# Second bias of the experts gathered into the output rows by an indirect DMA, in place of a matmul

## The chip, the cores and the metric

The kernel runs on one core of one Trainium2 chip. The metric is the device time of one execution in microseconds (us). Engines are named as in the profile: PE is TensorE's matmuls and PEld its weight loads, DVE is VectorE, ACT is ScalarE, POOL is GpSimd, SP is SyncE; a "q" behind a name (POOLq) is the engine's own queue of waits, register and DMA-issuing instructions.

## The reference, cut to what matters

1250 tokens of 1024 features go through a two-layer graph network (two SAGE layers over 40000 edges) and then through a feed-forward part with eight experts, of which each token takes the best two. The change lies in the last part:

```python
logits = jax.nn.silu(t @ rw1 + rb1) @ rw2 + rb2
vals, idx = jax.lax.top_k(logits, K)                       # K = 2 of E = 8 experts
w = jax.nn.softmax(masked, axis=1)                         # zero but for the two
eh = jax.nn.silu(jnp.einsum('td,edh->teh', t, ew1) + eb1[None])
eo = jnp.einsum('teh,ehd->ted', eh, ew2) + eb2[None]       # eb2: 8 x 1024, the second bias
y = t + jnp.einsum('te,ted->td', w, eo)
```

`x + y` is returned. So a token's row receives, for each of its two experts, w * (silu(t @ ew1 + eb1) @ ew2 + eb2). All is float32.

## The kernel before

**The first 925 us** are the graph network and the router: nearly all of it is matmuls, written with their own orders and buffers. The change touches it only where the second bias is prepared. In `routing_constants` (L266) eb2 is loaded as 64 x 128 values and split into three bfloat16 parts that add up to the float32 value (L297 and L299, three copies and two subtractions on DVE); each part is stored to a scratch tensor `eb2_d` in DRAM (L300). A constant `ones_b` of 3 x 128 ones is set (L302). Just before the experts start, the three parts are loaded into three partitions, `eb2_r` (L1599, on ACT's queue).

**The experts.** The 2 x 1250 (token, expert) pairs are sorted by expert into tiles of 128 slots, every tile of one expert; with this input there are 23 tiles. For each tile i there are two integer lists, `ids` (which token row each slot reads) and `to` (which output row it adds to), an expert number in `eid[:, i]`, the same in all partitions, and a weight per slot, `w_slot`. One tile goes through these steps:

- `gather(i)` (L1470): an indirect DMA from POOL reads the 128 token rows of 4 KB from `t_d` in DRAM into one of three buffers `xgs`.
- `fetch(i)` (L1481, L1482): PE turns the eight 128 x 128 blocks, ACT copies them from PSUM in two halves of 128 x 512.
- `first_layer(i)` (L1486 to L1498): PE and ACT load the expert number into a register (L1486), PE multiplies by ew1 (L1493), DVE copies the result (L1498).
- `second_layer(i)` (L1505 to L1529): PE turns the two halves of that result (L1505), ACT applies Silu with the first bias (L1507), and then for each half of the 1024 columns PE adds the bias by a matmul of `ones_b` with the three parts (L1514) and two products with ew2 (L1518) in one PSUM tile. The first half is weighted and copied out by ACT (L1524), the second by DVE (L1526), into one of two buffers `yos[i % 2]`. An indirect DMA from POOL adds the 128 rows to their rows of `out` in DRAM (L1529); below this is called the scatter of tile i.

The buffers `xgs`, `yos` and the turned tokens lie in columns of one large SBUF tensor L that the router has finished with. All indirect DMAs are issued by POOL in its own queue, one after the other. A scatter waits until the scatter before it has landed, since both add to `out`; and a tile's output buffer is written again two tiles later, when its scatter has landed.

**Order of the work.** `section` (L1543) writes, for each i, gather(i + 3), fetch(i + 1), first_layer(i), second_layer(i - 1). A scheduler may move instructions within each engine, and does: in the built kernel, in the regular stretch, PE goes first layer, the two turns of the tile before (L1505), its two bias matmuls (L1514), one turn of a token block, its second layer (L1518), the other seven turns. Each engine executes its own list in order. Tiles 0 to 19 are always there; tiles from 20 on lie in nested branches (`sections`).

The rest of the routing (`plan_rest`, L1419) is computed by DVE while tiles 0 to 2 run.

Of the kernel before, what the change touches and what calls it, by code (L numbers as in the profile page):

```python
# [13 lines left out]
BF = mybir.dt.bfloat16  # L14
I32 = mybir.dt.int32
AF = mybir.ActivationFunctionType
ALU = mybir.AluOpType
# [4 lines left out]
P = 128  # L22
# [6 lines left out]
def kernel(  # L29
# [21 lines left out]
    nc = tc.nc  # L51
    N, D = x.shape
    NE = src.shape[0]
    E, _, H = ew1.shape
    KD = D // P
    KH = H // P
# [22 lines left out]
    const = ctx.enter_context(tc.tile_pool(name="const", bufs=1))  # L79
    small = ctx.enter_context(tc.tile_pool(name="small", bufs=3))  # L80
    land = ctx.enter_context(tc.tile_pool(name="land", bufs=1))
    dram = ctx.enter_context(tc.tile_pool(name="dram", bufs=1, space=bass.MemoryType.DRAM))
    tpp = ctx.enter_context(tc.tile_pool(name="tpp", bufs=2, space=PSUM))
    t_d = dram.tile([NP, D], F32, name="t_d")
    v_d = dram.tile([NP, D], F32, name="v_d")
    eb2_d = dram.tile([3, E * D], BF, name="eb2_d")


    NT = KD * N
    WQ = KD * QW  # L90
    L = land.tile([P, NT + 4 * D + 2 * WQ], F32, name="L")
    hT1 = L[:, :NT].rearrange("p (k n) -> p k n", k=KD)
    SC = L[:, NT : NT + 4 * D]
    WW = L[:, NT + 4 * D :]
# [47 lines left out]
    stt = nc.vector.scalar_tensor_tensor  # L142
# [26 lines left out]
    at_iota = [9440]  # L169

    def iota(shape, pattern, mult=0):

        n = 1
        for d in shape[1:]:
            n *= d
        ti = L[: shape[0], at_iota[0] : at_iota[0] + n].bitcast(I32)
        at_iota[0] += n
        assert at_iota[0] <= NT - 320
        if len(shape) == 3:
            ti = ti.rearrange("p (a b) -> p a b", b=shape[2])  # L180
        nc.gpsimd.iota(ti, pattern=pattern, base=0, channel_multiplier=mult)
        return ti

    def counted(ti, name, dtype=F32):
        tf = const.tile(list(ti.shape), dtype, name=name)
        tc.keep_in_program_order(nc.vector.tensor_copy(tf, ti))
        return tf
# [76 lines left out]
    need = {}  # L264

    def routing_constants():  # L266
        late = tc.keep_in_program_order
        tiles = counted(tiles_i, "tiles")
        token = counted(token_i, "token")
        own_row = counted(own_row_i, "own_row")  # L270
        first = counted(first_i, "first")
        late(nc.vector.tensor_scalar(first, first, 0.0, None, op0=ALU.is_gt))

        lower = const.tile([P, P], F16, name="lower")
        late(nc.vector.tensor_scalar(lower, lane, own_row, None, op0=ALU.is_gt))
        ones = const.tile([P, P], F16, name="ones")
        late(nc.vector.memset(ones, 1.0))
        valid = const.tile([P, NB], F32, name="valid")
        late(nc.vector.tensor_scalar(valid, token, float(N), None, op0=ALU.is_lt))

        late(nc.vector.tensor_scalar(token, token, 1.0, None, op0=ALU.add))
        late(nc.vector.tensor_mul(token, token, valid))
        rb1_p = const.tile([P, KD], F32, name="rb1_p")
        late(nc.sync.dma_start(out=rb1_p, in_=rb1.rearrange("(k p) -> p k", p=P)))
        rb2_p = const.tile([E, 1], F32, name="rb2_p")
        late(nc.sync.dma_start(out=rb2_p, in_=rb2.rearrange("(e o) -> e o", o=1)))
        eb1_p = const.tile([P, E, KH], F32, name="eb1_p")
        late(nc.sync.dma_start(out=eb1_p, in_=eb1.rearrange("e (k p) -> p e k", p=P)))
        rw2_sb = const.tile([P, KD, E], F32, name="rw2_sb")
        late(nc.sync.dma_start(out=rw2_sb, in_=rw2.rearrange("(k p) e -> p k e", p=P)))  # L290

        ev = L[: E * D // P, NT - 320 : NT]
        eb2_f = ev[:, :P]
        late(nc.sync.dma_start(out=eb2_f, in_=eb2.rearrange("e (a n) -> (e a) n", n=P)))
        for i in range(3):
            part = ev[:, P + i * (P // 2) : P + (i + 1) * (P // 2)].bitcast(BF)
            late(nc.vector.tensor_copy(part, eb2_f))  # L297
            if i < 2:
                late(nc.vector.tensor_tensor(eb2_f, eb2_f, part, ALU.subtract))  # L299
            late(nc.sync.dma_start(out=eb2_d[i].rearrange("(a n) -> a n", n=P), in_=part))  # L300
        ones_b = const.tile([3, P], BF, name="ones_b")
        late(nc.vector.memset(ones_b, 1.0))  # L302
        lg = const.tile([P, NB, E], F32, name="lg")
        late(nc.vector.memset(lg, 0.0))
        need.update(
            tiles=tiles, token=token, first=first, lower=lower, ones=ones, valid=valid,
            rb1_p=rb1_p, rb2_p=rb2_p, eb1_p=eb1_p, rw2_sb=rw2_sb, ones_b=ones_b, lg=lg,
        )


# [696 lines left out]
    def moe():  # L1007
# [1 line left out]
        tiles, token, first, lower, ones, valid = (  # L1009
            need[k] for k in ("tiles", "token", "first", "lower", "ones", "valid")  # L1010
        )
        rb1_p, rb2_p, eb1_p, rw2_sb, ones_b, lg = (
            need[k] for k in ("rb1_p", "rb2_p", "eb1_p", "rw2_sb", "ones_b", "lg")
        )
        xwp = st.enter_context(tc.tile_pool(name="xwp", bufs=1, side="right"))
        xw = xwp.tile([P, E * WEXP], F32, name="xw")
# [42 lines left out]
        late = carver(SC[:, 512:1792])  # L1059
# [8 lines left out]
        def column(k):  # L1068
            return hT1[:, k, :TA]
# [3 lines left out]
        yos = [column(4 + i) for i in range(2)]  # L1073
# [12 lines left out]
        ids, to, eid = (keep([P, NTILE], I32) for _ in range(3))  # L1086
        w_slot = keep([P, NTILE])
# [375 lines left out]

        w1_all = xw.rearrange("p (e w) -> p e w", e=E)[:, :, : KD * H]
        w2_all = xw.rearrange("p (e w) -> p e w", e=E)[:, :, KD * H :]
        eb2_r = WW.bitcast(BF)[:3, : E * D]
        eb2_e = eb2_r.rearrange("i (e d) -> i e d", e=E)

        def gather(i):
            nc.gpsimd.indirect_dma_start(  # L1470
                out=xgs[i % 3], out_offset=None, in_=t_d[:N, :],
                in_offset=bass.IndirectOffsetOnAxis(ap=ids[:, i : i + 1], axis=0),
            )

        def fetch(i):
# [9 lines left out]
        def first_layer(i, xT):  # L1485
            e = nc.values_load(  # L1486
                eid[0:1, i : i + 1], engines=(ENG.PE, ENG.Activation),
                min_val=0, max_val=E - 1,
                skip_runtime_bounds_check_because="eid is a count of experts, cut at E - 1",
            )  # L1490
            ps = mm.tile([P, 512], F32, name="ps")
            for k in range(KD):
                nc.tensor.matmul(  # L1493
                    ps[:, :H], xT[:, k, :], w1_all[:, ds(e, 1), k * H : (k + 1) * H],
                    start=(k == 0), stop=(k == KD - 1),
                )
            hx = hxs[i % 2]
            nc.vector.tensor_copy(hx, ps[:, :H])  # L1498
            return e, hx

        def second_layer(i, e, hx):
            pt = tpp.tile([P, 4, P], F32, name="tp")
            hT = hTs[i % 2]
            for q in range(KH):
                nc.tensor.transpose(pt[:, q, :], hx[:, q * P : (q + 1) * P], ident)  # L1505
            for q in range(KH):
                nc.scalar.activation(  # L1507
                    hT[:, q, :], pt[:, q, :], AF.Silu, bias=eb1_p[:, ds(e, 1), q : q + 1]
                )
            yo = yos[i % 2]  # L1510
            for h in range(2):
                dc = slice(h * HALF, (h + 1) * HALF)
                ps = mm2.tile([P, 512], F32, name="ps2")
                nc.tensor.matmul(  # L1514
                    ps, ones_b, eb2_e[:, ds(e, 1), dc], start=True, stop=False
                )
                for q in range(KH):
                    nc.tensor.matmul(  # L1518
                        ps, hT[:, q, :],
                        w2_all[:, ds(e, 1), q * D + h * HALF : q * D + (h + 1) * HALF],  # L1520
                        start=False, stop=(q == KH - 1),
                    )
                if h == 0:
                    nc.scalar.activation(yo[:, dc], ps, AF.Copy, scale=w_slot[:, i : i + 1])  # L1524
                else:
                    nc.vector.tensor_scalar(  # L1526
                        yo[:, dc], ps, w_slot[:, i : i + 1], None, op0=ALU.mult
                    )
            nc.gpsimd.indirect_dma_start(  # L1529
                out=out[:, :],  # L1530
                out_offset=bass.IndirectOffsetOnAxis(ap=to[:, i : i + 1], axis=0),
                in_=yo, in_offset=None, bounds_check=N - 1, oob_is_err=False,
                compute_op=ALU.add,
            )
# [48 lines left out]
        for c in range(LAST):  # L1583
            logits(c)
        at_a, take_a = plan_first()
        gather(0)
        gather(1)
        gather(2)
        route(w2, 2, LAST)
# [6 lines left out]
        logits(LAST)  # L1596
        lgp.close()
        mm2 = st.enter_context(tc.tile_pool(name="mmy", bufs=3, space=PSUM))
        nc.scalar.dma_start(out=eb2_r, in_=eb2_d[:, :])  # L1599
        xTs[0] = fetch(0)  # L1600
        xTs[1] = fetch(1)
        held[0] = first_layer(0, xTs.pop(0))
        gather(3)
        section(1, 2, until=always)
# [52 lines left out]
```

## Time and profile before

| | |
|---|---|
| median of 3 runs | 1163.0 us (1160.78 to 1163.17) |
| the profiled execution | 1160.5 us |
| its span, first to last instruction | 1158.6 us |
| mean granted TensorE clock | 0.993 |
| PE busy | 1122.4 us, 97% of the span |
| POOL busy | 331.3 us, 29% |
| ACT busy | 181.5 us, 16% |
| first token gather issued | 924.97 us |
| last scatter issued | 1146.44 us |

Times in the profile count from the first instruction. A row of a group gives line, engine, operation, output<-inputs, shapes and the number of instructions, then busy us and mean ns of one, then the idle time of the engine just before them and what ended it. For a DMA on POOL the busy time is only that of POOL's own work of issuing it; the data moves later, and "to landing" is the time from the start of the issue until the transfer is complete. Matmuls overlap in the pipeline, so the mean duration of one is longer than the distance from one to the next. The line numbers are those of the kernel before.

### The profile page before, as it was taken

How to read it: one execution, taken by the hardware profiler on the slowest of the kernel's cores; microseconds unless marked ns; L12 is line 12 of the kernel's file. 1: busy time of each engine (PE TensorE's matmuls, PEld its weight loads, DVE VectorE, ACT ScalarE, POOL GpSimd, SP SyncE). 2: the span in 40 equal slices, each digit the busy share in tenths (PEclk: the TensorE clock that was granted, in tenths of full speed). 3: DMA queues.
4: the chain of work that ended last, by engine and by line, in shares of the span. 5: the costliest groups of instructions: out<-in, count | busy, mean ns of one | idle time of the engine just before them, and what ended most of it. 6: DMA issues, size and time to landing. Idle time of an engine off the chain costs nothing.

```text
span 1158.6 us, 13209 instructions
## 1 busy us (share of the span) xinstructions
PE 1122.4 (97%) x4775; PEld 789.3 (68%) x4775; DVE 452.2 (39%) x1127; ACT 181.5 (16%) x420; POOL 331.3 (29%) x438
## 2 busy tenths in 40 slices
PE   6999999999999999999999999999999989999994
PEld 4556556888888886887788688865333666666662
DVE  8767778751212164241234142555221532111110
ACT  5301000001111111100110000122111223222220
POOL 1899999700000000031004011540000013323221
PEclk9999999999999999999999999999999999999997
DMA  7011011010100021042014432347801435554542
GB/s 230 32 40 39 1 37 37 1 37 1 37 1 1 1 73 37 10 170 72 1 34 164 167 118 73 145 164 257 279 19 36 146 89 132 107 121 101 126 116 45
DMA packets 59330, 95.40 MB, mean 82 GB/s; under 512 B 8797, under 2 KB 35645, under 8 KB 59251
## 3 DMA queue, kind: packets, MB, share of 16 engines
q1 hardware_dynamic: 48400, 67.72, 17.0%
q0 software_dynamic: 7056, 23.88, 9.1%
q10 hardware_dynamic: 3798, 2.84, 0.8%
q8 instruction: 42, 0.69, 0.2%
q14 instruction: 34, 0.28, 0.1%
HBM read 68.76 MB, written 27.47 MB: 83 GB/s over the span
## 4 chain that ended last, share of the span: by engine, by line
PE 94%; DVE 2%; ACT 1%; DMA 1%; POOL 1%; issue 0%; ACTq 0%; DVEq 0%; POOLq 0%
PE ps L524 12%; PE ps L458 11%; PE psb L638 9%; PE ps L708 8%; PE ps L560 8%; PE ps L638 7%; PE ps L1493 7%; PE ps L1518 7%; PE ps L1173 5%; PE ps L625 5%; PE ps L1186 4%; PE cnt L419 3%; PE ps L1128 2%; PE tp L1481 2%; PE lg L1105 2%; PE ps L1514 1%
## 5 line engine op out<-in xcount | busy, mean ns | idle before, releaser
L409 POOL TENSOR_SCALAR ol<-lane,keys 125x128 f16<-125x128 f16 x320 | 192.1, 619 | 27.7 <-DVE oh L416 27.7
L458 PE MATMUL ps<-h0T,L 128*128 128x498 f32 (+2 forms) x384 | 147.6, 517 | 0.3 <-ACT h0T L321 0.2
L524 PE MATMUL ps<-L,h0T 128*128 128x256 f32 (+1 forms) x640 | 142.2, 379 | 0.0
L704 POOL TENSOR_TENSOR L<-L 128x512 f32<-128x512 f32 (+1 forms) x20 | 32.0, 1608 | 375.6 <-DVE L L617 217.6
L524 PEld LDWEIGHTS ps<-L,h0T 128*128 128x128 f32 (+1 forms) x640 | 118.3, 187 | 18.0 <-issue 0.6
L416 DVE TENSOR_SCALAR oh<-win,keys 125x240 f16<-125x240 f16 x320 | 85.7, 322 | 30.9 <-PE cnt L419 29.1
L458 PEld LDWEIGHTS ps<-h0T,L 128*128 128x128 f32 x384 | 67.5, 192 | 39.0 <-issue 33.9
L1493 PE MATMUL ps<-xw,L 128*128 x368 | 84.7, 383 | 0.3 <-issue 0.3
L1518 PE MATMUL ps<-xw,L 128*128 x184 | 83.5, 596 | 0.1
L560 PE MATMUL ps<-C,yh 128*128 128x256 f32 (+2 forms) x240 | 81.8, 356 | 0.0
L560 PE MATMUL ps<-C,yl 128*128 128x256 f32 (+2 forms) x240 | 81.5, 353 | 0.0
L708 PE MATMUL ps<-zh,C 128*128 128x512 f32 (+1 forms) x200 | 79.5, 398 | 0.0
L708 PE MATMUL ps<-zl,C 128*128 128x512 f32 (+1 forms) x200 | 78.6, 393 | 0.0
L1493 PEld LDWEIGHTS ps<-xw,L 128*128 128x128 f32 x368 | 69.0, 192 | 10.1 <-issue 1.4
L1529 POOL DMA_INDIRECT out_dram<-L x23 | 36.3, 1579 | 133.4 <-ACT L L1482 87.9
L1470 POOL DMA_INDIRECT L<-t_d,L x26 | 26.0, 1000 | 162.2 <-DVE L L140 142.2
L438 DVE TENSOR_TENSOR C<-C,cnt 128x240 f32 x160 | 64.4, 402 | 13.4 <-DVE oh L416 2.1
L1518 PEld LDWEIGHTS ps<-xw,L 128*128 128x128 f32 x184 | 33.2, 190 | 35.3 <-issue 33.0
L140 DVE TENSOR_TENSOR L<-L,ps 128x512 f32<-128x512 f32 (+1 forms) x28 | 17.1, 611 | 99.7 <-PE ps L1173 47.2
L419 PEld LDWEIGHTS <-ol 125*128 125x128 f16 x320 | 31.0, 97 | 36.6 <-POOL ol L409 21.7
L419 PE MATMUL cnt<-oh,ol 125*128 125x240 f16 x320 | 50.8, 265 | 2.5 <-POOL ol L409 2.1
L1526 DVE TENSOR_SCALAR L<-ps,L 128x512 f32<-128x512 f32 x23 | 17.3, 751 | 91.7 <-PE ps L1518 91.7
(224 smaller groups left out, 1516.6 us busy)
## 6 DMA issues: line engine op xcount, KB each, us to landing
xw<-in_L_ffn_ew_dram SPq DMA_DIRECT2D x16, 1024.0 KB, 7.6
L<-in_x_dram SPq DMA_DIRECT2D x20, 256.0 KB, 2.9
v_d<-L SPq DMA_DIRECT2D x18, 256.0 KB, 2.0
xa<-v_d SPq DMA_DIRECT2D x18, 256.0 KB, 5.9
t_d<-L SPq DMA_DIRECT2D x9, 512.0 KB, 4.4
out_dram<-xa SPq DMA_DIRECT2D x9, 512.0 KB, 4.0
L<-in_L_gnn_W_self_dram SPq DMA_DIRECT2D x4, 1024.0 KB, 5.7
L<-in_L_gnn_W_neigh_dram SPq DMA_DIRECT2D x4, 1024.0 KB
```

The source lines that it names most:

```text
L409: nc.gpsimd.tensor_scalar(ol[:, c, :], lane[:GP], keys[:, 1, c, r : r + 1], None, op0=ALU.is_equal)
L416: nc.vector.tensor_scalar(oh, win[:GP], keys[:, 0, i * GC + c, r : r + 1], None, op0=ALU.is_equal)
L419: nc.tensor.matmul(ps[:, i, :GW], ol[:, i * GC + c, :], oh, start=(c == 0), stop=(c == GC - 1),)
L438: nc.vector.tensor_tensor(to, to.bitcast(F32), ps[:, i, :GW].rearrange("p (k w) -> p k w", k=NB), ALU.add,)
L458: nc.tensor.matmul(ps[:, :n], w[:, k, (d % 2) * P : (d % 2 + 1) * P], h0T[:, k, c0 : c0 + n], start=(k == 0), stop=(k == KD - 1),)
L524: nc.tensor.matmul(ps[:m, :QW], hT[:, k, blk(b)], w[:, k, :], start=(k == 0), stop=(k == KD - 1))
L560: nc.tensor.matmul(ps[:, :n], part[: rows[k], k, (d % 2) * P : (d % 2 + 1) * P], C[: rows[k], k, c0 : c0 + n], start=(k == 0 and part is y ...
L625: nc.tensor.matmul(ps[:m], hT1[:, k, blk(b)], w[:, k, :], start=(k == 0), stop=(k == KD - 1))
L638: nc.tensor.matmul(ps, rows_of(k), w[:, k, :], start=(first and k == 0), stop=(k == KB - 1), skip_group_check=not first,)
L708: nc.tensor.matmul(ps[:m], C[: rows[k], k, blk(b)], part[: rows[k], k, :], start=(k == 0 and part is yh), stop=(k == NB - 1 and part is yl),)
L1493: nc.tensor.matmul(ps[:, :H], xT[:, k, :], w1_all[:, ds(e, 1), k * H : (k + 1) * H], start=(k == 0), stop=(k == KD - 1),)
L1518: nc.tensor.matmul(ps, hT[:, q, :], w2_all[:, ds(e, 1), q * D + h * HALF : q * D + (h + 1) * HALF], start=False, stop=(q == KH - 1),)
```

## The change

The second bias is no longer part of the matmul. For each tile, after the first layer is written, an indirect DMA from POOL (`gather_bias`) reads row eid of eb2 in DRAM, the same 4 KB row for all 128 slots, into the tile's output buffer `yos[i % 2]`. In `second_layer`, ACT multiplies that buffer by the slots' weights in place, 128 x 1024 values, ahead of the second layer's products. Both halves of the PSUM result are then weighted and added to the buffer by DVE (`stt`, one instruction for a half); ACT no longer copies a half out. The bias matmuls, the three bfloat16 parts with their load, stores and scratch tensor, `ones_b` and `eb2_r` are gone.

```diff
@@ routing_constants
-        ev = L[: E * D // P, NT - 320 : NT]
-        eb2_f = ev[:, :P]
-        late(nc.sync.dma_start(out=eb2_f, in_=eb2.rearrange("e (a n) -> (e a) n", n=P)))
-        for i in range(3):
-            part = ev[:, P + i * (P // 2) : P + (i + 1) * (P // 2)].bitcast(BF)
-            late(nc.vector.tensor_copy(part, eb2_f))
-            if i < 2:
-                late(nc.vector.tensor_tensor(eb2_f, eb2_f, part, ALU.subtract))
-            late(nc.sync.dma_start(out=eb2_d[i].rearrange("(a n) -> a n", n=P), in_=part))
-        ones_b = const.tile([3, P], BF, name="ones_b")
-        late(nc.vector.memset(ones_b, 1.0))
@@ moe
-        eb2_r = WW.bitcast(BF)[:3, : E * D]
-        eb2_e = eb2_r.rearrange("i (e d) -> i e d", e=E)
+        def gather_bias(i):
+
+            yo = yos[i % 2]
+            nc.gpsimd.indirect_dma_start(
+                out=yo, out_offset=None, in_=eb2[:, :],
+                in_offset=bass.IndirectOffsetOnAxis(ap=eid[:, i : i + 1], axis=0),
+            )
@@ first_layer
             nc.vector.tensor_copy(hx, ps[:, :H])
+            gather_bias(i)
             return e, hx
@@ second_layer
             yo = yos[i % 2]
+            nc.scalar.activation(yo, yo, AF.Copy, scale=w_slot[:, i : i + 1])
             for h in range(2):
                 dc = slice(h * HALF, (h + 1) * HALF)
                 ps = mm2.tile([P, 512], F32, name="ps2")
-                nc.tensor.matmul(
-                    ps, ones_b, eb2_e[:, ds(e, 1), dc], start=True, stop=False
-                )
                 for q in range(KH):
                     nc.tensor.matmul(
                         ps, hT[:, q, :],
                         w2_all[:, ds(e, 1), q * D + h * HALF : q * D + (h + 1) * HALF],
-                        start=False, stop=(q == KH - 1),
+                        start=(q == 0), stop=(q == KH - 1),
                     )
-                if h == 0:
-                    nc.scalar.activation(yo[:, dc], ps, AF.Copy, scale=w_slot[:, i : i + 1])
-                else:
-                    nc.vector.tensor_scalar(
-                        yo[:, dc], ps, w_slot[:, i : i + 1], None, op0=ALU.mult
-                    )
+                stt(yo[:, dc], ps, w_slot[:, i : i + 1], yo[:, dc], op0=ALU.mult, op1=ALU.add)
             nc.gpsimd.indirect_dma_start(
                 out=out[:, :],
...
@@ before the first tile
-        nc.scalar.dma_start(out=eb2_r, in_=eb2_d[:, :])
```

## The prediction

> **What bounds the kernel now.** First the page: the totals, then the chain that ended last.
>
> ```profile
> PE 1122.4 (97%) x4775; PEld 789.3 (68%) x4775; DVE 452.2 (39%) x1127; ACT 181.5 (16%) x420; POOL 331.3 (29%) x438
> PE 94%; DVE 2%; ACT 1%; DMA 1%; POOL 1%; issue 0%; ACTq 0%; DVEq 0%; POOLq 0%
> ```
>
> PE bounds the whole, so work taken from PE counts, and what others do is free until it makes PE wait. The change lies in the experts, so next I read the PE timeline of one regular tile there (start us, busy us, line, instructions).
>
> ```profile
> 1051.42 3.62 PE L1493 MATMUL ps<-xw,L 128*128 x16
> 1054.87 0.38 PE L1505 MATMUL tp<-ident,L 128*128 128x128 f32 x2
> 1055.19 0.60 PE L1514 MATMUL ps<-L,ones_b 3*128 x2
> 1055.72 0.33 PE L1481 MATMUL tp<-ident,L 128*128 128x128 f32 x1
> 1055.88 3.60 PE L1518 MATMUL ps<-xw,L 128*128 x8
> 1059.32 0.93 PE L1481 MATMUL tp<-ident,L 128*128 128x128 f32 x7
> 1060.09 2.11 PE L1493 MATMUL ps<-xw,L 128*128 x9
> ```
>
> A tile takes 1060.09 - 1051.42 = 8.67 us. The bias matmuls (L1514) take 0.53 us of it, up to 1055.72, but they stand where PE waits for Silu of the turned block (L1505). Then POOL's timeline and the DMA issues: what its queue does in the same period, and how long a transfer takes from issue to landing (last column).
>
> ```profile
> 1052.36 1.57 POOL L1529 DMA_INDIRECT out_dram<-L  x1 [5.79 <-ACT L L1482]
> 1054.24 1.00 POOL L1470 DMA_INDIRECT L<-t_d,L  x1 [0.30 <-issue]
> 1061.03 1.57 POOL L1529 DMA_INDIRECT out_dram<-L  x1 [5.79 <-ACT L L1482]
> ```
>
> ```profile
> L<-in_L_gnn_b_dram SPq DMA_DIRECT2D x1, 512.0 KB, 3.7
> L<-t_d,L POOLq DMA_INDIRECT x26, 5.6
> out_dram<-L POOLq DMA_INDIRECT x23, 6.0
> ```
>
> POOL works 2.6 us of 8.67 and looks idle. It isn't free: a scatter lands 6.0 us after its issue began, and the next may not start before. There are 2.7 us of slack in that loop, and nobody but the next scatter waits for it. The queue's own row for the scatters' second wait agrees (ns, min/median/max, first and last start):
>
> ```profile
> L1529 POOLq EVENT_SEMAPHORE  x7: 1687/1957/3434, 1004.9 to 1058.5; - x7
> ```
>
> The last of these starts at 1058.5: there the landing of the scatter of 1052.36 has been seen, 6.1 us after.
>
> **The change, part by part.**
>
> Removed from PE: 46 bias matmuls. In the built kernel PE's order becomes L1505, four turns, second layer, four turns, first layer. One tile before has that order already (L1493 to L1481 around 1112.98 to 1121.42): L1505 to L1518 0.90 us, L1518 to the turns 3.54, four turns 0.44, first layer 3.46, in all 8.34 us. So the gain is 0.33 us a tile, not 0.53; over some 18 regular tiles 6 us, if nothing else bounds.
>
> Removed early: three copies and two subtractions of 64x128 on DVE (276 ns each), a memset, four DMAs from SP, and before the experts one load on ACT. At 107 us PE is busy in nine tenths or more, and nothing there waits for them. I count 0; if DVE's 1.4 us were on the path, 1 us. SP's next weight load leaves earlier (now at 110.11) but its data is used from about 150 us: 0.
>
> Moved from ACT to DVE: the first half's copy-out (L1524, 687 ns). The nearest row for the new instruction is the same operation in the graph network:
>
> ```profile
> L712 DVE SCALAR_TENSOR_TENSOR L<-ps,dinv_p,L x20: 737/751/754, 502.7 to 653.1; 128x512 f32<-128x512 f32 x18, 98x512 f32<-98x512 f32 x2
> ```
>
> 751 ns, as L1526 now. DVE is idle some 7 us of each tile: hidden, and the end of a tile (second half out, then scatter) keeps its length: from L1518's start to the scatter 1061.03 - 1055.88 = 5.15 us. In tiles 0 and 1, where DVE plans the rest of the routing, the extra half lies between planning steps, while one matmul of the ranks comes earlier: 0, bounds -2 and +1.
>
> Added on ACT: one scaling of 128x1024. ACT's activations take 418 ns for 256 and 621 for 498 columns (L569), 0.84 ns a column; from 722 ns for 512 columns out of SBUF (L1117) that is 722 + 430 = 1.15 us.
>
> Added on POOL: one indirect DMA a tile, 1.0 us of issue as L1470, plus 0.3 between two. This is what decides, for its place. `gather_bias(i)` writes the buffer that scatter i-2 reads, so it waits until that scatter has landed. In the built kernel POOL's list in the regular stretch is: scatter i-2, bias i, token gather, scatter i-1, bias i+1, and so on. The wait for the landing, which only the next scatter had, now stands in front of the token gather and the scatter too.
>
> Loop 1, POOL alone: landing 6.0, wake 0.3 (a token gather starts 0.28 after the ids it waits for), bias 1.0, 0.3, token gather 1.0, 0.3 to the next scatter: 8.9 us. A scatter now follows two gathers of 512 KB directly, where before it came first; in the trace, gather and scatter keep the DMA engines busy about 5 of 8.67 us. So its landing may be later by 0 to 1.2 us; I take 0.5: 9.4 us a tile.
>
> Loop 2, over two tiles: scatter to landing 6.5, wake 0.3, the bias lands, then ACT. On ACT the order from tile 6 on is: first half of a token block, scaling of i, load of the expert number, second half, Silu of i. So the scaling holds up the copy and Silu behind it, PE's next turns (they wait for that copy), and the second layer. Behind the bias's landing: 0.1, scaling 1.15, load 0.38 (L1486: 0.28, and the step to it), copy 0.59 (L1482), 0.55 to the second layer (0.44 of turns and the step), 5.15 to the scatter: 7.9 us.
>
> Landing of the bias: L1470 gives 4.0 at least, 5.6 in the median, 6.4 at most. All slots read one row; the broadcast of b1 (512 KB from one 4 KB row, 3.7 us) shows no penalty for that. The median is of gathers behind a scatter; the bias has none ahead, but a gather behind: I take 5.0, ends 4.0 and 6.4.
>
> Loop 2 is 6.5 + 0.3 + 5.0 + 7.9 = 19.7 us for two tiles, 9.85 a tile. It is the longer one.
>
> Here a rule speaks otherwise. The Trainium skill, "DMA: Bandwidth & Descriptors", section "Anatomy of one DMA — SWDGE (gpsimd) path", puts a DMA issued by GpSimd at 2.0 us plus bytes / 436e3. For 512 KB that is 3.2 us, an estimate from the page. With it loop 1 is 3.2 + 2.9 = 6.1 and loop 2 (3.2 + 0.3 + 3.2 + 7.9) / 2 = 7.3 a tile: both under 8.34, the bias would be hidden and the kernel 6 us faster. The trace has 5.6 and 6.0 for these very transfers (rows of 4 KB by index, the scatter adding in DRAM), so I take the trace.
>
> The sum, against scatter starts of before. Scatter 1 stays at 967.1. Scatter 2: 967.1 + 9.4 = 976.5 (was 975.1). Scatter 3: 985.9. To scatter 16 13 x 9.85: 1114.0 (was 1095.7), +18.3. To scatter 18 two more: 1133.7 (was 1112.3), +21.4. Scatter 19 has bias 20 and three token gathers ahead: 6.5 + 0.3 + 4 x 1.3 = 12.0 (was 10.8): +22.6. Scatter 20: 8.1 later: +22.8. Scatters 21 and 22 hang on loop 2 without load and copy, 18.7 us behind 19 and 20: 1172.5 (was 1146.4), +26. The 12.2 us behind the last scatter stay. Minus 1 for the early parts and for the ranks: +25. The profiled execution took 1160.5, its span and 1.9 us around it, and would come to 1185.5; it lies 2.5 under the median of the runs, so the median becomes 1163.0 + 25 = 1188.
>
> Ends: bias 4.0 and no contention give 9.1 a tile and +11 (1174). Bias 6.4, landing 7.2 and 0.75 of wake (what a scatter takes from seen landing to start, 1145.7 to 1146.44) give 11.1 a tile and +50 (1213).
>
> **The rivals.**
>
> The bias is hidden (10%): PE sets 8.34 a tile, 1163 - 6 = 1157, faster. It decides at this point: the bias has to be in SBUF about 8.8 us after scatter i-2 started (two tiles of 8.34 less the 7.9 behind it), and it can't be issued before 6.3. It would have to land in 2.5 us. Against it: no indirect DMA of the trace took under 4.0. For it: the page's 3.2, and the 3.7 of the broadcast, with a landing of 4.5 that single scatters reach.
>
> The indirect transfers get in each other's way (10%): a third stream of 512 KB goes from one queue, all readings from one row of DRAM. If bias and scatter both take 2 us longer than I took, loop 2 is 23.7, 11.9 a tile, and the sum about +57: 1220. For it: at least one token gather is always in flight beside the bias. Against: the DMA engines were busy only half the time, and 1.7 us more a tile do not fill them.
>
> Likeliest (80%): POOL's wait for the landing sets the pace, 1174 to 1207.
>
> **How the numbers follow.** 0.2% of 1163 is 2.3 us, about what a measurement of this kernel can tell from no change. Faster by more: 0.09, nearly the first rival. Within: 0.03, where loops come out at 8.5 to 8.7. Slower: 0.88. The range 1173 to 1207 leaves out both rivals in the main. Time 1188.
>
> **What would show it.** Right: scatters 9 to 10.6 us apart from tile 6 on; POOL's bias row idle before it some 5 us with the DMA of the scatter as releaser; ACT's scaling waiting for the bias's DMA; PE's idle before L1518 up, in all by some 25 us, though PE's busy time falls by 14. Wrong: PE without gaps and 8.3 us a tile (hidden), or bias landings of 7 us and more (contention). If scaling never waits but scatters are over 9 us apart, loop 1 rules and loop 2 is wrong.

## The result: 4% slower, and the profile after

| | before | after |
|---|---|---|
| median | 1162.2 us (4 runs, 1160.8 to 1163.2) | 1209.5 us (4 runs, 1206.4 to 1212.5) |
| ratio | | 1.041, 95% interval 1.037 to 1.044 |
| the profiled execution, its span | 1160.5, 1158.6 us | 1212.5, 1210.0 us |
| mean granted TensorE clock | 0.993 | 0.975 |

The forecast was 1188 us, with a range of 1173 to 1207. The sign and the place were right: POOL's wait for the landing, in the experts. The size was not: +47 us in place of +25, outside the range. Up to the first indirect DMA of the experts (924.3 us, before 925.0) nothing has changed.

The page of after, totals and the chain that ended last:

```profile
PE 1129.0 (93%) x4729; PEld 795.2 (66%) x4729; DVE 466.9 (39%) x1144; ACT 189.6 (16%) x420; POOL 354.2 (29%) x461
PE 82%; DMA 7%; issue 4%; ACT 2%; POOL 2%; DVE 2%; ACTq 0%; POOLq 0%; DVEq 0%
```

DMA has come into the chain, from 1% to 7%. And PE's busy time did not fall by the 14 us of the bias matmuls; it rose by 7, though PE does less. The reason comes further down. First POOL's timeline of two tiles (start us, busy us, line; in brackets the idle time ahead and what ended it). L1516 is now the scatter, L1463 the bias, L1455 the token gather.

```profile
1046.54 1.61 POOL L1516 DMA_INDIRECT out_dram<-L  x1 [0.30 <-issue]
1053.57 0.98 POOL L1463 DMA_INDIRECT L<-in_L_ffn_eb_dram,L  x1 [5.42 <-DMA out_dram<-L]
1058.80 0.94 POOL L1455 DMA_INDIRECT L<-t_d,L  x1 [4.25 <-PE tp L1474]
1060.04 1.61 POOL L1516 DMA_INDIRECT out_dram<-L  x1 [0.30 <-issue]
```

The bias waits 5.4 us for the scatter's landing, as forecast. But then the token gather waits 4.25 us more, for PE's turns (L1474), and the next scatter stands behind it: 13.5 us from scatter to scatter, where 9.85 were forecast. What PE and ACT did meanwhile (rows of PE and ACT in the same timeline; L1505 is the scaling, L1475 the copies, L1499 and L1474 the turns, L1510 the second layer):

```profile
1047.62 0.38 PE L1499 MATMUL tp<-ident,L 128*128 128x128 f32 x2
1049.27 1.15 ACT L1505 ACTIVATE L<-L 128x1024 f32<-128x1024 f32 x1 [8.40 <-DMA L<-in_L_ffn_eb_dram,L]
1050.47 0.58 ACT L1475 COPY L<-tp 128x512 f32<-128x512 f32 x1
1051.11 1.12 PE L1474 MATMUL tp<-ident,L 128*128 128x128 f32 x4 [3.10 <-ACT L L1475]
1052.02 6.07 PE L1510 MATMUL ps<-xw,L 128*128 x8
1057.92 0.60 PE L1474 MATMUL tp<-ident,L 128*128 128x128 f32 x4
```

ACT stands for 8.4 us in front of the scaling, whose bias has not landed. The copy behind it is late, PE idles 3.1 us, and then the same second layer that takes 3.70 us in the next tile takes 6.07, and four turns 1.12 in place of 0.60: the granted TensorE clock is 0.50 from 1050.2 to 1057.0 us. That is the busy time that PE gained (the second layer 100.1 us in all, before 83.5). Such slow tiles alternate with quick ones; over the regular stretch the granted clock is 0.90 (column PEclk, third from the end):

```profile
985.00:1125.00 140.00, 117.97 (x438) 77.09 (x437) 25.05 (x39) 35.25 (x64) 45.08 (x39) 0.90 0.55 138
```

Scatter starts, span ends and their shifts, by the profiled executions (us):

| | before | after | shift | forecast |
|---|---|---|---|---|
| scatter 16 | 1095.7 | 1125.8 | +30.1 | +18.3 |
| scatter 18 | 1112.3 | 1146.1 | +33.8 | +21.4 |
| scatter 19 | 1123.1 | 1165.9 | +42.8 | +22.6 |
| scatter 22, the last | 1146.4 | 1190.7 | +44.3 | +26 |
| end of the span | 1158.6 | 1210.0 | +51.4 | +25 |

The profiled execution of after is the slowest of its four and that of before a quick one (1160.5 us), so the spans are 51 us apart and the medians 47. Three things are missing in the forecast: 12 us in the regular stretch, 8 us from scatter 18 to 19 (19.8 us, forecast 12.0), where the branch for tile 20 begins, and 7 us behind the last scatter (19.3 us, forecast 12.2). From scatter 19 to 22 it is 2 us less than forecast. At the branch one scaling stands 6.9 us, and a token gather 10.1 us, with scatter 19 behind it (rows of ACT and POOL):

```profile
1155.26 1.15 ACT L1505 ACTIVATE L<-L 128x1024 f32<-128x1024 f32 x1 [6.88 <-DMA L<-in_L_ffn_eb_dram,L]
1164.62 0.94 POOL L1455 DMA_INDIRECT L<-t_d,L  x1 [10.08 <-PE tp L1474]
1165.86 1.61 POOL L1516 DMA_INDIRECT out_dram<-L  x1 [0.30 <-issue]
```

### The profile page after: what moved, and what is told of

It is laid out like the page before. It is cut to its first block, busy times and chain, and to the rows that moved or that the text cites. A ratio compares the mean times of both kernels' runs of the same rounds, so it can differ in the third digit from the quotient of the medians.

```text
span 1210.0 us, 13100 instructions
## 1 busy us (share of the span) xinstructions
PE 1129.0 (93%) x4729; PEld 795.2 (66%) x4729; DVE 466.9 (39%) x1144; ACT 189.6 (16%) x420; POOL 354.2 (29%) x461
## 4 chain that ended last, share of the span: by engine, by line
PE 82%; DMA 7%; issue 4%; ACT 2%; POOL 2%; DVE 2%; ACTq 0%; POOLq 0%; DVEq 0%
PE ps L511 11%; PE ps L445 10%; PE psb L625 9%; PE ps L695 8%; PE ps L547 8%; PE ps L625 7%; PE ps L1510 5%; PE ps L1160 5%; PE ps L612 5%; PE ps L1173 4%; DMA L<-in_L_ffn_eb_dram,L 3%; DMA out_dram<-L 3%; PE cnt L406 3%; PE ps L1486 2%; PE ps L1115 2%
## 5 line engine op out<-in xcount | busy, mean ns | idle before, releaser
L1510 PE MATMUL ps<-xw,L 128*128 x184 | 100.1, 695 | 12.8 <-ACT L L1501 12.3
L1463 POOL DMA_INDIRECT L<-in_L_ffn_eb_dram,L x23 | 22.6, 982 | 242.6 <-DVE L L139 133.6
L1486 PE MATMUL ps<-xw,L 128*128 x368 | 84.4, 381 | 1.5 <-issue 1.5
L1515 DVE SCALAR_TENSOR_TENSOR L<-ps,L 128x512 f32<-128x512 f32 x46 | 34.4, 751 | 123.5 <-PE ps L1510 119.8
L1510 PEld LDWEIGHTS ps<-xw,L 128*128 128x128 f32 x184 | 39.8, 227 | 59.5 <-issue 43.0
L1486 PEld LDWEIGHTS ps<-xw,L 128*128 128x128 f32 x368 | 68.1, 191 | 11.4 <-issue 3.4
L406 PEld LDWEIGHTS <-ol 125*128 125x128 f16 x320 | 30.9, 97 | 37.6 <-POOL ol L396 19.7
L1474 PE MATMUL tp<-ident,L 128*128 128x128 f32 x184 | 30.1, 295 | 26.1 <-ACT L L1475 25.9
L377 DVE TENSOR_TENSOR yl<-ps,yh 128x256 fp32r<-128x256 f32 (+1 forms) x40 | 17.0, 424 | 94.0 <-ACT yh L376 94.0
```

The source lines that it names most:

```text
L406: nc.tensor.matmul(ps[:, i, :GW], ol[:, i * GC + c, :], oh, start=(c == 0), stop=(c == GC - 1),)
L1486: nc.tensor.matmul(ps[:, :H], xT[:, k, :], w1_all[:, ds(e, 1), k * H : (k + 1) * H], start=(k == 0), stop=(k == KD - 1),)
L1510: nc.tensor.matmul(ps, hT[:, q, :], w2_all[:, ds(e, 1), q * D + h * HALF : q * D + (h + 1) * HALF], start=(q == 0), stop=(q == KH - 1),)
```

## The experiments

My theory before the first of them: the wait for the scatter's landing, and what is queued behind it on POOL and ScalarE, is the whole cost; the half clock is a part that I left out. The rivals: the third stream of 512 KB a tile costs by itself, or the scaling does. One table for all runs: "pace" is the mean distance of scatters 3 to 16, "18 to 19" the step at the branch, "tail" the time from the last scatter's start to the end of the span. These three come from one profiled execution of each kernel, which lies up to 5 us from the kernel's median (e2 and e9 below it, e8 above), so a few tenths of a microsecond in the pace of the slow kernels tell nothing.

| kernel | median us | ratio to before (95%) | pace | 18 to 19 | tail |
|---|---|---|---|---|---|
| before | 1162 | | 8.66 | 10.8 | 12.2 |
| after | 1209.5 | 1.041 (1.037 to 1.044) | 10.85 | 19.8 | 19.3 |
| e1 four buffers | 1208.4 | 1.041 (1.039 to 1.044) | 10.82 | 19.9 | 19.6 |
| e2 scaling on DVE | 1201.5 | 1.034 (1.033 to 1.036) | 9.75 | 12.6 | 19.0 |
| e3 before without bias matmuls | 1152.4 | 0.992 (0.990 to 0.993) | 8.34 | 10.0 | 12.6 |
| e4 filler matmuls | 1208.2 | 1.039 (1.038 to 1.041) | 10.62 | 20.1 | 20.6 |
| e5 four buffers, pinned | 1159.0 | 0.999 (0.997 to 1.000) | 8.34 | 9.4 | 19.1 |
| e6 scaling pinned | 1195.0 | 1.029 (1.027 to 1.031) | 10.34 | 11.4 | 19.7 |
| e7 no late bias | 1212.8 | 1.043 (1.041 to 1.046) | 11.06 | 19.9 | 14.8 |
| e8 64 KB bias | 1198.9 | 1.031 (1.028 to 1.033) | 10.06 | 17.9 | 19.9 |
| e9 POOL pinned | 1191.5 | 1.027 (1.023 to 1.031) | 9.20 | 17.7 | 19.1 |
| e10 both pinned | 1161.5 | 1.000 (0.999 to 1.001) | 8.42 | 8.2 | 19.1 |
| e11 bias from SyncE | 1153.4 | 0.992 (0.990 to 0.994) | 8.39 | 7.9 | 12.3 |
| e12 the same, four buffers | 1152.5 | 0.991 (0.990 to 0.993) | 8.30 | 9.0 | 12.0 |

**e1: four output buffers.**

```diff
-        yos = [column(4 + i) for i in range(2)]
+        yos = [column(4 + i) for i in range(2)] + [WW[:, i * D : (i + 1) * D] for i in range(2)]
... (in gather_bias and in second_layer)
-            yo = yos[i % 2]
+            yo = yos[i % 4]
```

> Four output buffers instead of two, so that the bias of tile i waits for the scatter of tile i-4 and not of i-2; the number of transfers, their sizes and the scaling on ScalarE stay. If the wait for the scatter's landing (and what it does to ScalarE, TensorE and its clock) is the whole cost: tiles 8.3 us apart, no TensorE idle over 1 us in the regular stretch, clock 0.99, 1157 to 1163 us. If the third stream of 512 KB a tile itself is the cost (contention): landings of 7 us and more stay, 1180 us or more.

Neither: 1208.4 us, nothing gained. The rows of waits in the regular stretch (engine and line, what it waited for: us in all, times, longest) read as in after:

```profile
ACT L L1505 <- DMA L<-in_L_ffn_eb_dram,L: 88.0, 13, 9.2
POOL L L1463 <- DMA out_dram<-L: 76.7, 13, 6.6
```

The built order says why. The scheduler used the two new buffers to issue each bias, and each scaling, two tiles earlier: four biases now stand ahead of scatter 0, and then the bias of tile i + 4 directly behind scatter i, for whose landing it waits. A buffer more did not move the wait; it moved the instruction. The run says nothing against the wait, and nothing for the rival.

**e2: the scaling on VectorE.**

```diff
-            nc.scalar.activation(yo, yo, AF.Copy, scale=w_slot[:, i : i + 1])
+            nc.vector.tensor_scalar(yo, yo, w_slot[:, i : i + 1], None, op0=ALU.mult)
```

> The scaling of the bias by the slots' weights moved from ScalarE to VectorE, two buffers as before: the wait for the landing stays on POOL, but it no longer holds up ScalarE's copies and Silu, and so not TensorE's turns. If my two loops are right: loop 2 is 6.5 + 0.3 + 4.5 + some 3.5 behind it = 14.8 us for two tiles and rules no more; POOL's own loop of 9.4 us a tile rules, TensorE's idle is cut into pieces of about 1 us and the clock stays at 0.99: about 1178 us (1172 to 1184). If the transfers themselves are the cost, or the half clock comes from something else than ScalarE's delay: 1200 us or more. If POOL's loop isn't one: 1160.

1201.5, 17 us over the expected range, for the most part not in the regular stretch: scatter 16 is 17.6 us late, and the pace is 9.75 where 9.4 was expected. I had not counted the tail, 7 us, and the tiles in the branches (12 us more from scatter 16 to 22). With ScalarE free the step at the branch falls from 19.8 to 12.6 us. Taking the scaling off ScalarE so gives some 1.1 us a tile and 7 us at the branch; the rest of the slow pace is left.

**e3: the gain on TensorE alone.**

```diff
-                nc.tensor.matmul(
-                    ps, ones_b, eb2_e[:, ds(e, 1), dc], start=True, stop=False
-                )
...
-                        start=False, stop=(q == KH - 1),
+                        start=(q == 0), stop=(q == KH - 1),
```

> The kernel before with only the bias matmuls left out; nothing takes their place, so the second bias is missing from the output. It measures the gain on TensorE alone. By the prediction 0.33 us for each of some 18 regular tiles: 6 us, 1156 us. If the turns that take their place wait as well: no change, 1162. If the matmuls' whole busy time comes free: 0.6 x 23 = 14 us, 1148.

A tile takes 8.33 us (second layer to second layer in PE's timeline, 1058.08 - 1049.75), where 8.34 were worked out:

```profile
1049.75 3.70 PE L1515 MATMUL ps<-xw,L 128*128 x8
1053.28 0.60 PE L1481 MATMUL tp<-ident,L 128*128 128x128 f32 x4
1053.72 3.62 PE L1493 MATMUL ps<-xw,L 128*128 x16
1057.18 0.38 PE L1505 MATMUL tp<-ident,L 128*128 128x128 f32 x2
1057.39 0.60 PE L1481 MATMUL tp<-ident,L 128*128 128x128 f32 x4
1058.08 3.70 PE L1515 MATMUL ps<-xw,L 128*128 x8
```

In all it is 9 us faster; 2.8 of them come before scatter 1, in the tiles beside the routing, which I had counted as 0. This is what a free bias would be worth.

**e4: TensorE kept busy.**

```diff
+            idle = mm2.tile([P, 512], F32, name="ps2")
+            for _ in range(2):
+                nc.tensor.matmul(idle, hx[:, :P], xw[:, :512], start=True, stop=True)
```

> The changed kernel with two more matmuls in each tile, whose products are never read, behind the first layer and ahead of the turns (about 0.9 us each at full clock). If the clock gate is what my sum lacked: TensorE's idle before the turns falls from 3.0 to 3.6 us to under 2, the second layer takes 3.6 to 3.7 us in every tile instead of 4.7 to 6.1 in every other one, two tiles take about 20.3 us (TensorE's 16.7 + 3.6) instead of 22.3, the mean clock is 0.99 and the kernel is faster than the changed one by 10 to 18 us, 1192 to 1200, though it does more work. If the clock is only a symptom, and the wait on POOL sets the pace alone: 1209, no change. If TensorE's work counts in full: 1209 + 1.8 x 20 = 1245.

The clock does what I expected: 1.00 in the regular stretch, and a second layer of 3.6 to 3.7 us in every tile.

```profile
985.00:1125.00 140.00, 131.22 (x505) 83.91 (x504) 25.05 (x39) 35.95 (x66) 47.48 (x41) 1.00 0.59 144
```

The time does not: 1208.2, not told apart from 1209.5; the pace is 10.62 in place of 10.85. Another loop stands right behind, POOL's own (L1519 is the scatter here): scatters are 10.7 us apart, most of it the wait for the landing.

```profile
1089.17 0.98 POOL L1463 DMA_INDIRECT L<-in_L_ffn_eb_dram,L  x1 [6.56 <-DMA out_dram<-L]
1090.45 0.94 POOL L1455 DMA_INDIRECT L<-t_d,L  x1 [0.30 <-issue]
1091.70 1.61 POOL L1519 DMA_INDIRECT out_dram<-L  x1 [0.30 <-issue]
```

So the half clock is real, but with POOL's order as it is almost nothing hangs on it.

**e5: four buffers, with the order kept.** The bias gather and the scaling pinned behind what is written ahead of them on their engine, with the buffers of e1:

```diff
-            nc.gpsimd.indirect_dma_start(
+            tc.keep_in_program_order(nc.gpsimd.indirect_dma_start(
                 out=yo, out_offset=None, in_=eb2[:, :],
...
-            nc.scalar.activation(yo, yo, AF.Copy, scale=w_slot[:, i : i + 1])
+            tc.keep_in_program_order(
+                nc.scalar.activation(yo, yo, AF.Copy, scale=w_slot[:, i : i + 1])
+            )
```

> Four output buffers, and the bias gather and the scaling each pinned behind what is written ahead of them on their engine: on POOL the bias of tile i+2 stands ahead of scatter i and waits for scatter i-2 (not for the one just issued), on ScalarE the scaling of tile i stands behind the Silu of tile i. Bytes and work are those of the changed kernel. If the places of the waits in the in-order queues are the cause: no TensorE idle over 1 us, 8.33 us a tile as without the bias, the last scatter near 1139, and with the longer stretch behind the last scatter that all kernels with the gathers had so far (19 us instead of 12) 1157 to 1161 us, level with the kernel before. If the third stream of 512 KB is itself too much for the queue (the landing of a scatter over 8.3 us when two gathers run beside it): 9 us a tile and more, 1175 us or more.

1159.0 us, as expected, and the pace of e3. POOL's timeline: the bias follows a scatter at once, and waits for nothing:

```profile
1054.73 1.62 POOL L1518 DMA_INDIRECT out_dram<-L  x1 [0.30 <-issue]
1056.65 0.98 POOL L1463 DMA_INDIRECT L<-in_L_ffn_eb_dram,L  x1 [0.30 <-issue]
1061.82 0.94 POOL L1455 DMA_INDIRECT L<-t_d,L  x1 [4.19 <-PE tp L1474]
```

The same bytes go over in less time (175 GB/s in the stretch, after has 138). The rival of the third stream is refuted; what differs from e1, which has the same four buffers, is the order in POOL's and ScalarE's queues. The 7 us by which it stays behind e3 are the tail.

**e6: only the scaling pinned,** two buffers, POOL's order as in after (the second hunk of e5 alone).

> The changed kernel with only the scaling pinned behind the Silu of its own tile on ScalarE; two buffers, POOL's order as in the changed kernel. Tells ScalarE's hold-up from POOL's. If the two loops are separate: ScalarE's copies no longer wait, no half clock, POOL's own loop of 7.3 + 2.5 = 9.8 us a tile is left, and the tail of 19 us: 1195 to 1201, as with the scaling on VectorE. If ScalarE's order were the whole cost: 1160. If neither: 1209.

1195.0, as expected, and the step at the branch is 11.4 us. What is left is mainly POOL's own loop (L1518 is the scatter in this kernel, as in e5):

```profile
1043.87 1.61 POOL L1518 DMA_INDIRECT out_dram<-L  x1 [0.30 <-issue]
1051.86 0.98 POOL L1463 DMA_INDIRECT L<-in_L_ffn_eb_dram,L  x1 [6.39 <-DMA out_dram<-L]
1053.14 0.94 POOL L1455 DMA_INDIRECT L<-t_d,L  x1 [0.31 <-issue]
1054.39 1.61 POOL L1518 DMA_INDIRECT out_dram<-L  x1 [0.30 <-issue]
```

From scatter to bias 7.7 us in the mean of the stretch, 1.28 to the token gather, 1.25 to the scatter: 10.2 us. I had 9.4. The token gather no longer waits for PE's turns (0.3 us in all in the stretch, in after 16.5). The half clock did not go away, as I had expected: the granted clock in the stretch is 0.94.

**e7: code that is never run.**

```diff
-            gather_bias(i)
+            if i < ends[0]:
+                gather_bias(i)
```

> The changed kernel without the bias gathers of tiles 23 to 26, which lie in branches that this input never takes. What is executed is the same, but the branch that is skipped holds 5 DMAs instead of 9. If the longer stretch behind the last scatter comes from the skipped branch's semaphores (its exit waits for all eight of the queue's semaphores in the changed kernel, the last scatter's among them, and for five of them in the kernel before): the stretch falls from 19.3 to 12 to 14 us, 1202 to 1204 us. If it comes from the last scatter's own late landing or anything that is executed: 1209, 19 us.

The total missed: 1212.8 us. The tiles themselves ran at 11.06 us, and the last scatter was 6 us later than in after; POOL's order there is the same. The intervals of the two kernels' ratios overlap (1.041 to 1.046 and 1.037 to 1.044), and why the tiles of this execution are slower is open. The tail is what the run was for, and it fell from 19.3 to 14.8 us. POOL's queue at the branch, after first, then e7 (durations in ns, first and last start in us):

```profile
L1549 POOLq EVENT_SEMAPHORE  x4: 17/43/43, 1190.7 to 1195.8; - x4
L1549 POOLq INC_SWDGE_SEM  x1: 1620/1620/1620, 1195.9 to 1195.9; - x1
```

```profile
L1550 POOLq EVENT_SEMAPHORE  x2: 43/43/43, 1196.6 to 1196.7; - x2
L1550 POOLq INC_SWDGE_SEM  x1: 1624/1624/1624, 1196.8 to 1196.8; - x1
```

In after POOL waits at the branch until 1195.8, 5.1 us behind the start of the last scatter (1190.70); in e7 it goes on 0.2 us after the scatter of 1196.64 began. In the built kernels, the exit of the skipped branch settles the semaphores of the DMAs that the branch would have issued, and waits for them first. With the biases these are nine DMAs, and POOL waited until the last scatter had landed, 5.1 us after its start; without them they are five, as in the kernel before, and it did not. So 4.5 us of the tail come from DMAs that are not issued. The rest is bookkeeping: INC_SWDGE_SEM, of which there are two in the tail, takes 1.62 us (before 1.18), and POOL's last drain 5.96 (before 4.08).

**e8: fewer bytes.**

```diff
-                out=yo, out_offset=None, in_=eb2[:, :],
+                out=yo[:, :P], out_offset=None, in_=eb2.rearrange('e (a n) -> (e a) n', n=P),
```

> The changed kernel with the bias gather reading 128 of the 1024 columns (512 bytes a slot, 64 KB instead of 512 KB); the other columns of the buffer keep old values, so the bias is missing there. Waits, order and number of transfers stay. If the bytes count: the bias lands in 2 to 3.5 us instead of 4.6, the scatter in 6.0 instead of 6.8; the two tiles' chain falls by 2 x 0.8 + 2 and tiles come at 9 to 9.4 us: 1175 to 1188. If each indirect transfer has mainly a fixed cost: landings within 0.5 us of those of the changed kernel, 1200 us or more.

1198.9, near what a fixed cost would give (1200 or more; by the bytes 1175 to 1188). An eighth of the bytes shortens the way from the bias's issue to the scaling from 4.64 to 3.81 us, and leaves the way from scatter to bias at 7.0 (after 7.1). Most of this gather's time isn't its bytes.

**e9: only POOL's order pinned.** The three indirect DMAs in the order written (token gather, bias, scatter), as in e5's first hunk for each of them; scaling free, two buffers.

> The changed kernel (two buffers, scaling left where the scheduler puts it) with POOL's transfers kept in the order written: after scatter i-2 first the token gather, which waits for nothing, then the bias of tile i, then scatter i-1. The token gather is so issued while the scatter lands. If the two loops are separate: POOL's loop falls from about 10.2 to 7.7 + 1.3 = 9.0 us, the chain over two tiles through ScalarE (measured 7.1 + 4.6 + 3.1 + 5.2 to 6.8) is left alone: 10.0 to 10.4 us a tile, 1190 to 1198 with the tail of 19 us. If POOL's loop alone set the pace: 9 us, 1172. If the order on POOL doesn't matter: 1209.

1191.5, as expected. In the regular stretch it does better than that, 9.20 us a tile. The token gather now goes out while the scatter lands, and POOL's loop is short; ScalarE's chain is alone (rows of POOL, ACT and PE):

```profile
1048.44 1.61 POOL L1516 DMA_INDIRECT out_dram<-L  x1 [2.19 <-issue]
1050.36 0.98 POOL L1455 DMA_INDIRECT L<-t_d,L  x1 [0.30 <-issue]
1055.07 0.94 POOL L1463 DMA_INDIRECT L<-in_L_ffn_eb_dram,L  x1 [3.73 <-DMA out_dram<-L]
1059.29 1.15 ACT L1505 ACTIVATE L<-L 128x1024 f32<-128x1024 f32 x1 [6.41 <-DMA L<-in_L_ffn_eb_dram,L]
1061.46 3.60 PE L1510 MATMUL ps<-xw,L 128*128 x8
1066.65 1.62 POOL L1516 DMA_INDIRECT out_dram<-L  x1 [2.04 <-issue]
```

From 1048.44 to 1066.65 the chain is walked through: 6.63 to the bias, 4.22 to the scaling, 2.17 to the second layer, 5.19 to the scatter two tiles on. Means of the stretch: 6.45 + 4.57 + 2.14 + 5.26 = 18.4 us. PE idles under 2 us at a time, and the clock is 1.00. At the branch, where the scheduler has put scalings ahead of the copies, the step of 17.7 us is still there.

**e10: both pinned,** two buffers.

> As the run with POOL's order pinned, and the scaling pinned behind the Silu of its tile as well; still two buffers, the same bytes. Both loops are then eased: 9.0 us a tile on POOL, the chain (7.7 + 4.9 + 1.3 + 1.5 + 0.3) / 2 = 7.9. If the two loops are the whole cost: 8.6 to 9.1 us a tile, last scatter at 1142 to 1152, 1161 to 1172 with the tail. If a third loop or the bytes were behind it: over 9.5 us a tile, 1180 or more.

1161.5 us, at the lower edge of what was expected; the pace of 8.42 and the last scatter at 1137.7 are better than expected, and the tail of 19 us remains. The scatter's landing is still waited for, and nobody minds (waits of the regular stretch; L1501 is Silu, L1506 the scaling):

```profile
POOL L L1463 <- DMA out_dram<-L: 65.8, 17, 5.2
ACT L L1501 <- PE tp L1499: 55.5, 17, 5.5
...
ACT L L1506 <- DMA L<-in_L_ffn_eb_dram,L: 12.3, 8, 3.1
```

POOL waits as long in all as in after (66.9 us there, in 12 waits), but what stands behind the wait isn't needed yet; ScalarE waits for PE again. The same instructions, buffers and bytes as in after, in another order: 48 us.

**e11 and e12: the bias from SyncE's queue,** with two and with four buffers, scaling pinned. The expert number is loaded into a register of SyncE too.

```diff
-            nc.gpsimd.indirect_dma_start(
-                out=yo, out_offset=None, in_=eb2[:, :],
-                in_offset=bass.IndirectOffsetOnAxis(ap=eid[:, i : i + 1], axis=0),
-            )
+            nc.sync.dma_start(out=yo, in_=eb2[ds(e, 1), :].to_broadcast([P, D]))
```

> The bias row fetched by a plain DMA from SyncE's queue (the expert number in a register, one 4 KB row to all 128 partitions) in place of POOL's gather; two buffers, scaling pinned. SyncE waits for the landing of scatter i-2 and nothing stands behind it there; POOL has its two transfers of before. If the cost is the wait in POOL's and ScalarE's queues, and the tail comes from the number of POOL's transfers: 8.33 us a tile, 12.5 us behind the last scatter as without any bias, 1152 to 1155, faster than both kernels. If the transfer itself costs (512 KB beside gather and scatter): 1160 or more.

> As the bias from SyncE's queue, with four output buffers. If two buffers are enough once nothing is queued behind the wait: the same within 2 us. If the bias still lands too late with two (scatter's landing 7.5 + 3.7 + scaling 1.2 + rest 2 = 14.4 us of the 16.7 of two tiles): this one is faster by up to 5 us.

1153.4 and 1152.5 us: both 0.8 to 0.9% faster than the kernel before, 4.6 to 4.7% faster than the changed one, and level with e3, which has no second bias at all (1152.4); their intervals overlap, so two buffers are enough. The landings in e11's regular stretch (median us):

```profile
L<-in_L_ffn_eb_dram SPq DMA_DIRECT2D x17, 512.0 KB, 4.8
L<-t_d,L POOLq DMA_INDIRECT x16, 6.5
out_dram<-L POOLq DMA_INDIRECT x16, 7.7
```

The bias is no quicker than by POOL's gather, and token gather and scatter land later than in before (5.7 and 6.0). All of it is hidden, since on SyncE nothing is queued behind the wait, though it is a long one:

```profile
SPq L1463 <- DMA out_dram<-L: 110.4, 15, 9.5
```

The tail is 12.3 us again.

## Why the prediction was right in kind and wrong in size

Right, by its steps:

- **The gain on PE.** 8.34 us a tile worked out, 8.33 measured (e3).
- **Single instructions.** Scaling 1.15 us, the two weighted additions 751 ns each, the bias's issue 0.98, as taken. Landing of the bias 4.5 to 4.6 in the median, 5.0 taken, within the ends.
- **Loop 2.** Its sum was 6.5 + 0.3 + 5.0 + 7.9 = 19.7 us for two tiles. Where it is alone (e9) it measures 18.4, term by term as set out: 6.45, 4.57, 2.14 and 5.26.
- **The rule weighed against the trace.** The Trainium skill's 2.0 us plus bytes / 436e3 ("DMA: Bandwidth & Descriptors", "Anatomy of one DMA — SWDGE (gpsimd) path") would have hidden the bias, by the estimate from the page; the trace does not follow it. e8 tells which part of it doesn't carry over: 448 KB less save 0.83 us where the slope gives 1.05, but 64 KB still need 3.8 us to the scaling's start, where the page gives 2.15.

Wrong, and where the 26 us lie that the forecast lacked: 12 in the regular stretch (loop 1, the rule for two loops, the clock), 8 at scatter 19, 7 behind the last scatter, less 2 made good between.

- **"8.9 us ... I take 0.5: 9.4 us a tile" (loop 1).** The term is landing and wake, 6.8 with the 0.5 for contention. Alone (e6) it measures 7.7, and the loop 10.2. With bias and token gather issued in the 2.5 us ahead of it, the scatter lands later: median 7.4 to 7.7 us in e6, 6.4 in e9, where only the bias is directly ahead; before 6.0.
- **"It is the longer one" (loop 2).** It is the shorter: 9.2 a tile against 10.2. And taking the longer of the two is not enough. In after they run through each other: a late copy (loop 2) makes PE's turns late, these hold the token gather, and the scatter behind it is in loop 1. The chain over two tiles is there 7.11 + 4.64 + 3.13 + 6.80 = 21.7 us; the last term, from second layer to scatter, was 5.15 in the sum. Undoing one loop alone gives 10.34 (e6) and 9.20 (e9), both together 8.42 (e10). This is 13 tiles x 1.0 us; scatter 3 was 1 us earlier than forecast, so 12 us lack at scatter 16.
- **TensorE's clock** was not in the sum at all. Gaps of 3 us and more in PE, as in the rows above, were followed by matmuls at half clock, and shorter ones went either way: 2.4 us in after did it, and 2.0 to 2.5 five times in e8, but 2.7 in e1 did not. The length of one gap does not decide. Read in steps of 0.1 us, the granted clock of after, e1, e2, e6, e7 and e8 is at 0.50 for 3.41 us or twice that, and in each of these runs all such stretches start a whole multiple of 3.41 us apart. Between 985 and 1130 us there are 28 of them; in the 3.41 us ahead of the start PE was idle for 1.8 us or more every time, and the windows after which the clock stayed full had 2.0 at most. So idle time adds up within windows of 3.41 us, and the same gap counts or not by where it falls among them. The Trainium skill, "TensorE: Matmul & The Clock Gate", "What's actually happening", has a rule for this: after an idle window of about 3.4 us, which runs freely, the clock falls to a half. The trace agrees in the window and its free running; but a window idle for little more than half was enough. By e4 little of the 10.85 us a tile hangs on it: with full clock the pace was 10.62, POOL's loop standing behind. What it would cost where POOL does not bind, no run shows.
- **"Scatter 19 ... 12.0"**: 19.8. I counted POOL's issues there, and not ACT: at the branch's start the scaling of tile 20 stands ahead of a copy that the turns for the third token gather need. In after that gather waits 10.1 us, and scatter 19 stands behind it. With the scaling pinned the step is 11.4 (e6) and 8.2 (e10), with POOL alone pinned 17.7 (e9): ScalarE's order is shown as the cause.
- **"The 12.2 us behind the last scatter stay"**: 19.3, by the skipped branch (e7: 4.5 us) and the longer bookkeeping of POOL's DMAs (with the bias on SyncE the tail is back at 12.3).

Of the rivals, the hidden bias was possible all along, with the price that the rival named (1157; e10 1161, e5 1159): what it lacked was not a quicker landing but another order, and the longer tail took back what the matmul gave. The rival of contention (1220) comes near the measured time for the wrong reason: e5 and e10 move the same bytes in the same number of transfers without the loss. The upper end of the forecast's own working (1213) covers the measured time too, but by luck: it took 6.4 us for the bias's landing, which measured 4.5.

Open stay how the 10.85 us split between the half clock and the coupling of the loops, and the slower tiles of e7.

## What to carry to other kernels

Before a transfer is added to an in-order queue, ask what it waits for and what stands behind it there: with the same 23 gathers the change came out 47 us slower when each stood directly behind the scatter whose buffer it reuses, and level when the independent gather was put ahead and the consumer kept behind its own tile's work; with the bias as a plain transfer on a queue in which nothing stands behind it, the change brought 8 us. More buffers don't help while a scheduler is free to spend them on issuing earlier; fix the order first. When two loops through the same queue come out within a few per cent of each other, don't take the longer one as the pace: forecast above both. And look at TensorE's idle time for the clock: here some 2 us within 3.41 were enough to halve it.

## What the runs showed of the hardware that I had not expected

- A branch that is not taken costs time for the DMAs in it: with nine in place of five in the skipped branch POOL had to wait for the last scatter's landing, 4.5 us (after and e7).
- The number of columns matters little to the gather of the bias into 128 partitions: 3.8 us from issue to use with 64 KB (e8), 4.6 with 512 KB (after).
- VectorE scales 128 x 1024 values between SBUF buffers in 0.75 us (e2), as long as for 128 x 512 out of PSUM with an addition; ScalarE takes 1.15.
